# Eight 64 KB weight transfers on two queues in place of one 512 KB transfer ahead of the activations

## The chip, the core and the metric

The kernel runs on one core of a Trainium2 chip. The metric is the device time of one launch in microseconds: 327.43 us, the median of 3 runs (327.39 to 327.58).

## What is computed

There are 128 samples `x[b]` of 128 channels by 1024 time steps, eight weight matrices of 128 by 128, and for each sample an index that chooses one of the eight. Each sample is multiplied by its matrix and added to the product; everything is float32.

```python
# x: (128, 128, 1024); subjects: (128,) of 0..7; weights: (8, 128, 128)
w = weights[subjects]
out = x + jnp.einsum('bct,bcd->bdt', x, w)
```

The input is 67.1 MB of samples and 0.5 MB of weights, the output 67.1 MB.

## The kernel before, in words

The work goes in 64 tiles of `G = 2` samples. A tile lies in one of `SLOTS = 23` slots of the on-chip memory, each 1 MB (`xs`), is multiplied into one of two PSUM buffers (`ps`), and the sum is written over the sample itself, from where it is stored. The order is written out by hand with semaphores, engine by engine:

- **SyncE (SP) issues the loads**, on its own DMA queue (q1 in the profile). Its first transfer is `w_all`, all eight matrices in one (L148): the matrix index becomes the middle dimension on the chip, so that each piece of the transfer is one matrix row, 512 bytes. Then the loop at L149 issues each sample as a transfer of 512 KB (L158, inside the helper `transfer`, whose instruction is at L59). `ROWS = 4` makes each piece read four neighbouring rows, 16 KB. Tiles 0 to 2 are issued at once; from tile 3 (`LEAD = 3`) SP first waits until the tile three before has landed (L155, L156), and from tile 23 until the slot's former tile has been stored (L152, L153). At the end SP waits for the last stores (L222).
- **ScalarE (ACT) issues** the index vector `given` (L127) as its first transfer, and later all stores (L212 to L217), on its own DMA queue (q10). It does nothing else.
- **VectorE (DVE)** fills `zeros` (L129), brings the indices into range (L139 to L143), and for every tile adds product and sample (L210).
- **GpSimd (POOL)** reads the indices, waits once for `w_all` (L186: `s_wall` at 16, since each transfer adds 16 to its semaphore), and copies the chosen matrix of every sample to one of four small buffers (L189). The copy of a tile from the third on waits for the tile's load as well (L193).
- **TensorE (PE)** starts with `IDLE = 3` multiplications of zeros (L132), which are recorded as six. Each sample then is two multiplications of 512 columns (L199). Tile 0 is done as two single samples, so that the first one can begin when sample 0 has landed; it has a semaphore of its own, `s_first`.

The loads, the stores and the index vector all share the core's 16 DMA engines.

Of the kernel before, what the change touches and what calls it, by code (L numbers as in the profile page):

```python
# [36 lines left out]
DMA = 16  # L40
# [7 lines left out]
ROWS = 4  # L48
# [3 lines left out]
def transfer(nc, engine, out, in_):  # L52

    later, nc._always_lower_symbolic_ap = nc._always_lower_symbolic_ap, False
    ins, outs = engine.lower_ap_dma(in_), engine.lower_ap_dma(out)
    nc._always_lower_symbolic_ap = later
    return engine.add_instruction(  # L59
        mybir.InstDMACopy(  # L60
            name=nc.get_next_instruction_name(),
            engine=engine.engine,
            ins=ins,
            outs=outs,
            mode="Copy",
            cce_op=ALU.bypass,
            queue=QUEUES[engine.engine],
        )
    )


@with_exitstack
def kernel(
    ctx: ExitStack,
    tc: tile.TileContext,
    x: bass.AP,
    subjects: bass.AP,
    weights: bass.AP,
    out: bass.AP,
):  # L80
    nc = tc.nc
    B, C, T = x.shape
    S, _, D = weights.shape
    NT = B // G

    def sbuf(name, *shape, dtype=F32):
        return ctx.enter_context(nc.sbuf_tensor(name, list(shape), dtype)).ap()

    given, near, wrap, index = (
        sbuf(name, 1, B, dtype=I32) for name in ("given", "near", "wrap", "index")  # L90
    )
    w_all = sbuf("w_all", C, S, D)
    ws = [sbuf(f"w{i}", C, 1, D) for i in range(W_SLOTS)]
    zeros = sbuf("zeros", C, N)
    xs = [sbuf(f"x{i}", C, G, T) for i in range(SLOTS)]
    ps = [
        ctx.enter_context(nc.psum_tensor(f"ps{i}", [D, G, T], F32)).ap() for i in range(P_SLOTS)
    ]

    s_given = tc.alloc_semaphore("s_given")  # L100
    s_wall = tc.alloc_semaphore("s_wall")
    s_index = tc.alloc_semaphore("s_index")
    s_zeros = tc.alloc_semaphore("s_zeros")
    s_copied = tc.alloc_semaphore("s_copied")
    s_product = tc.alloc_semaphore("s_product")
    s_added = tc.alloc_semaphore("s_added")
    s_slot = [tc.alloc_semaphore(f"s_slot{i}") for i in range(SLOTS)]


    s_first = tc.alloc_semaphore("s_first")  # L110

    def loaded(i):

        k, turn = i % SLOTS, i // SLOTS
        if i == 0:
            return [(s_first, DMA), (s_slot[0], DMA)]
        return [(s_slot[k], TURN * turn + DMA * G - (TURN - 2 * DMA if k == 0 else 0))]

    def stored(i):

        if i == 0:
            return [(s_first, 2 * DMA), (s_slot[0], 2 * DMA)]
        return [(s, count + DMA) for s, count in loaded(i)]

    with tc.tile_critical():  # L125

        nc.scalar.dma_start(given, subjects.rearrange("(o b) -> o b", o=1)).then_inc(s_given, DMA)  # L127

        nc.vector.memset(zeros, 0.0).then_inc(s_zeros, 1)  # L129
        nc.tensor.wait_ge(s_zeros, 1)  # L130
        for _ in range(IDLE):
            nc.tensor.matmul(  # L132
                ps[P_SLOTS - 1][:, G - 1, :N], zeros[:, :D], zeros, start=True, stop=True
            )

        nc.vector.wait_ge(s_given, DMA)
        nc.vector.tensor_scalar(near, given, -S, S - 1, ALU.max, ALU.min).then_inc(s_index, 1)  # L139
        nc.vector.wait_ge(s_index, 1)  # L140
        nc.vector.tensor_scalar(wrap, near, 0, S, ALU.is_lt, ALU.mult).then_inc(s_index, 1)  # L141
        nc.vector.wait_ge(s_index, 2)
        nc.vector.tensor_tensor(index, near, wrap, ALU.add).then_inc(s_index, 1)  # L143
        nc.gpsimd.wait_ge(s_index, 3)

        nc.sync.dma_start(w_all, weights.rearrange("s c d -> c s d")).then_inc(s_wall, DMA)  # L148
        for i in range(NT):  # L149
            k = i % SLOTS  # L150
            if i >= SLOTS:
                for s, count in stored(i - SLOTS):  # L152
                    nc.sync.wait_ge(s, count)  # L153
            elif i >= LEAD:
                for s, count in loaded(i - LEAD):  # L155
                    nc.sync.wait_ge(s, count)  # L156
            for g in range(G):
                transfer(  # L158
                    nc,
                    nc.sync,  # L160
                    xs[k][:, g, :],
                    x[i * G + g].rearrange("(a r) t -> a (r t)", r=ROWS),
                ).then_inc(s_first if i + g == 0 else s_slot[k], DMA)


        units = [(0, g, g + 1) for g in range(G)] + [(i, 0, G) for i in range(1, NT)]
        for u, (i, g0, g1) in enumerate(units):
            k = i % SLOTS
            p = ps[i % P_SLOTS]

            if i < P_SLOTS:
                nc.tensor.wait_ge(*loaded(i)[g0])
            for g in range(g0, g1):
                b = i * G + g
                if b % R == 0:
                    _, subject = nc.values_load_multi_w_load_instructions(  # L178
                        index[0:1, b : b + R],
                        engines=[mybir.EngineType.Pool],  # L180
                        min_val=0,
                        max_val=S - 1,
                        skip_runtime_bounds_check_because="the index is clamped on the chip above",
                    )
                if b == 0:
                    nc.gpsimd.wait_ge(s_wall, DMA)  # L186
                if i >= P_SLOTS and g == g0:
                    nc.gpsimd.wait_ge(s_added, u - P_SLOTS + 1)
                copy = nc.gpsimd.tensor_copy(  # L189
                    ws[b % W_SLOTS], w_all[:, bass.ds(subject[b % R], 1), :]  # L190
                )
                if i >= P_SLOTS and g == g0:
                    copy.wait_op(*loaded(i)[0], "sem-ge")  # L193
            copy.then_inc(s_copied, 1)

            nc.tensor.wait_ge(s_copied, u + 1)
            for g in range(g0, g1):
                for t in range(0, T, N):
                    mm = nc.tensor.matmul(  # L199
                        p[:, g, t : t + N],  # L200
                        ws[(i * G + g) % W_SLOTS][:, 0, :],
                        xs[k][:, g, t : t + N],
                        start=True,
                        stop=True,
                    )
            mm.then_inc(s_product, 1)

            mine = xs[k][:, g0:g1, :]
            nc.vector.wait_ge(s_product, u + 1)
            nc.vector.tensor_tensor(mine, p[:, g0:g1, :], mine, ALU.add).then_inc(s_added, 1)  # L210
            nc.scalar.wait_ge(s_added, u + 1)
            transfer(  # L212
                nc,
                nc.scalar,
                out[i * G + g0 : i * G + g1].rearrange("g d t -> d g t"),
                mine.rearrange("d (o g) t -> d o (g t)", o=1),
            ).then_inc(s_first if u == 0 else s_slot[k], DMA)  # L217


        for i in range(NT - SLOTS, NT):  # L220
            for s, count in stored(i):
                nc.sync.wait_ge(s, count)  # L222
# [27 lines left out]
```

## Time and profile before

| | before |
|---|---|
| median of the runs | 327.43 us (327.39 to 327.58) |
| the profiled execution: own time, span from first to last instruction | 327.13 us, 325.4 us |
| PE, DVE, POOL busy | 240.0, 148.0, 34.3 us |
| DMA | 134.85 MB, mean 414 GB/s |
| `w_all`: issue, time to issue, from issue to landing | at 0.97 us, 0.44 us, 4.3 us |
| first four samples: issue starts | 1.46, 2.08, 2.71, 3.35 us |
| median packet on a DMA engine: 512 bytes, 4 KB, 8 KB, 16 KB | 27, 159, 311, 616 ns |

The first rows are the page's and the times'. The issue starts come from the timeline, the packet rows from the trace's record of every DMA packet: a packet is one contiguous piece of a transfer, and it belongs to one of the 16 engines. The profile was taken on one execution, whose own time lies 0.3 us under the median; 1.7 us of it lie outside its span.

### The profile page before, as it was taken

To read this page: it belongs to the slowest core of one execution; us is meant where nothing else is said; L and a number is where in the kernel's file an instruction comes from. 1 tells how busy PE (TensorE), PEld (TensorE's weight loads), DVE (VectorE), ACT (ScalarE), POOL (GpSimd) and SP (SyncE) were. 2 spreads that over 40 slices of the span, in tenths; PEclk is the share of its full clock that TensorE was granted. 3 is DMA by queue.
4 is the path that set the end of the run, shared out by engine and by line. 5 is a ranking of instruction groups with operands and counts; after the bars stand their busy time and mean duration, and the time that the engine had idled before them with its cause. 6 is when DMAs were issued, how large, how long until landed. Compare 5 with 4: busy or idle time off the path is not lost.

```text
span 325.4 us, 1637 instructions
## 1 busy us (share of the span) xinstructions
PE 240.0 (74%) x518; PEld 94.3 (29%) x518; DVE 148.0 (45%) x69; POOL 34.3 (11%) x132
## 2 busy tenths in 40 slices
PE   7999978989999989889889889887866867000000
PEld 3344323333333333333333333332322322000000
DVE  1466654555555555555555555555254453100000
POOL 1011111111111111111111111111011010000000
PEclk9999999999999999999999999999999999655555
DMA  7999999999999999999999999999999999999994
GB/s 258 401 426 431 419 428 418 421 425 425 427 427 423 421 430 422 426 425 423 426 421 423 422 431 419 429 420 431 421 430 427 418 424 426 425 429 423 428 425 203
DMA packets 16554, 134.85 MB, mean 414 GB/s; under 512 B 3105, under 2 KB 4130, under 8 KB 4386
## 3 DMA queue, kind: packets, MB, share of 16 engines
q1 hardware_dynamic: 7184, 67.64, 49.7%
q10 hardware_dynamic: 9362, 67.11, 49.2%
q8 instruction: 4, 0.07, 0.1%
q14 instruction: 4, 0.03, 0.0%
HBM read 67.63 MB, written 67.11 MB: 414 GB/s over the span
## 4 chain that ended last, share of the span: by engine, by line
PE 39%; DVE 21%; issue 17%; POOL 4%; DMA 2%; POOLq 1%; SPq 1%
PE ps L199 39%; DVE x L210 21%; POOL w L189 4%; DMA x<-in_x_dram 2%; POOLq L189 1%; SPq L59 1%; POOLq L178 0%; SPq L148 0%; SPq L246 0%; SPq L125 0%
## 5 line engine op out<-in xcount | busy, mean ns | idle before, releaser
L199 PE MATMUL ps<-x,w 128*128 128x512 f32 x512 | 235.2, 604 | 34.1 <-POOL w L189 33.2
L210 DVE TENSOR_TENSOR x<-ps,x 128x2048 f32<-128x2048 f32 (+1 forms) x65 | 146.8, 2259 | 128.2 <-PE ps L199 128.2
L199 PEld LDWEIGHTS ps<-x,w 128*128 128x128 f32 x512 | 92.5, 189 | 176.8 <-issue 91.8
L189 POOL COPY w<-w_all 128x128 f32 x128 | 34.1, 296 | 237.4 <-DMA x<-in_x_dram 220.6
L132 PE MATMUL ps<-zeros 128*128 128x512 f32 x6 | 4.7, 956 | 1.7 <-DVE zeros L129 1.7
L132 PEld LDWEIGHTS ps<-zeros 128*128 128x128 f32 x6 | 1.9, 329 | 3.7 <-issue 2.1
L129 DVE MEMSET zeros<- 128x512 f32 x1 | 0.5, 485 | 1.1 <-SPq L125 1.1
L139 DVE TENSOR_SCALAR near<-given 1x128 int32<-1x128 int32 x1 | 0.2, 215 | 0.6 <-DMA given<-in_itok_B_dram 0.6
L143 DVE CUSTOM_DVE_ANT_0 index<-near,wrap 1x256 uint16<-1x256 uint16 x1 | 0.3, 281 | 0.0
L141 DVE TENSOR_SCALAR wrap<-near 1x128 int32<-1x128 int32 x1 | 0.2, 216 | 0.0
L237 POOL MEMSET const-float32-0.0<- 128x1 f32 x1 | 0.1, 99 | 0.2 <-issue 0.2
L237 POOL MEMSET const-bfloat16-1.0<- 128x1 bf16 x1 | 0.1, 102 | 0.0
L237 POOL MEMSET const-uint8-127<- 128x1 uint8 x1 | 0.1, 102 | 0.0
L237 POOL MEMSET const-float32-1.0<- 128x1 f32 x1 | 0.1, 99 | 0.0
## 6 DMA issues: line engine op xcount, KB each, us to landing
x<-in_x_dram SPq DMA_DIRECT2D x128, 512.0 KB, 11.8
out_dram<-x ACTq DMA_DIRECT2D x63, 1024.0 KB, 41.6
out_dram<-x ACTq DMA_DIRECT2D x2, 512.0 KB, 11.3
w_all<-in_L_cond_weights_dram SPq DMA_DIRECT2D x1, 512.0 KB, 4.3
given<-in_itok_B_dram ACTq DMA_DIRECT2D x1, 0.5 KB
```

The lines of the kernel that those rows point to most:

```text
L59: return engine.add_instruction(mybir.InstDMACopy(name=nc.get_next_instruction_name(), engine=engine.engine, ins=ins, outs=outs, mode="Cop ...
L129: nc.vector.memset(zeros, 0.0).then_inc(s_zeros, 1)
L132: nc.tensor.matmul(ps[P_SLOTS - 1][:, G - 1, :N], zeros[:, :D], zeros, start=True, stop=True)
L139: nc.vector.tensor_scalar(near, given, -S, S - 1, ALU.max, ALU.min).then_inc(s_index, 1)
L141: nc.vector.tensor_scalar(wrap, near, 0, S, ALU.is_lt, ALU.mult).then_inc(s_index, 1)
L143: nc.vector.tensor_tensor(index, near, wrap, ALU.add).then_inc(s_index, 1)
L189: copy = nc.gpsimd.tensor_copy(ws[b % W_SLOTS], w_all[:, bass.ds(subject[b % R], 1), :])
L199: mm = nc.tensor.matmul(p[:, g, t : t + N], ws[(i * G + g) % W_SLOTS][:, 0, :], xs[k][:, g, t : t + N], start=True, stop=True,)
L210: nc.vector.tensor_tensor(mine, p[:, g0:g1, :], mine, ALU.add).then_inc(s_added, 1)
L237: nc = _bacc.Bacc("TRN2", target_bir_lowering=False, num_devices=1)
```

## The change

The one transfer of `w_all` on SP's queue (L148) goes. A helper `load_matrix` moves one matrix, with pieces of four rows (2 KB) on the side that is read. Matrices 4 to 7 are issued by ACT, directly after the index vector. Matrices 0 to 3 are issued by SP, between sample 0 and sample 1, so that sample 0 is now SP's first transfer. All eight count on `s_wall`, and POOL's wait before its first copy asks for all of them.

```diff
+    def load_matrix(engine, m):
+        transfer(
+            nc,
+            engine,
+            w_all[:, m, :],
+            weights[m].rearrange("(a r) d -> a (r d)", r=ROWS),
+        ).then_inc(s_wall, DMA)
+
     with tc.tile_critical():
 
         nc.scalar.dma_start(given, subjects.rearrange("(o b) -> o b", o=1)).then_inc(s_given, DMA)
+        for m in range(S // 2, S):
+            load_matrix(nc.scalar, m)
...
-        nc.sync.dma_start(w_all, weights.rearrange("s c d -> c s d")).then_inc(s_wall, DMA)
         for i in range(NT):
...
                 ).then_inc(s_first if i + g == 0 else s_slot[k], DMA)
+                if i + g == 0:
+                    for m in range(S // 2):
+                        load_matrix(nc.sync, m)
...
-                    nc.gpsimd.wait_ge(s_wall, DMA)
+                    nc.gpsimd.wait_ge(s_wall, DMA * S)
```

## The prediction

> **What bounds the kernel now.** I read the page's slices first, then its DMA queues, then the DMA share in short stretches at both ends, then the waits.
>
> ```profile
> DMA  7999999999999999999999999999999999999994
> GB/s 258 401 426 431 419 428 418 421 425 425 427 427 423 421 430 422 426 425 423 426 421 423 422 431 419 429 420 431 421 430 427 418 424 426 425 429 423 428 425 203
> ...
> q1 hardware_dynamic: 7184, 67.64, 49.7%
> q10 hardware_dynamic: 9362, 67.11, 49.2%
> ```
>
> The 16 DMA engines are full from the second slice to the last. Loads (q1) and stores (q10) together take 98.9% of 16 engines' time: 0.989 x 325.4 = 321.8 us of 325.4. Only 3.6 us per engine are left. The page's chain of waits names PE (39%) and DVE (21%), but PE has 240.0 us of work and DVE 148.0; the chain crosses them because each tile must pass them, while tiles come as fast as the DMA brings them. So I count everything in DMA time. Where are the 3.6 us?
>
> ```profile
> 1.50:2.00 0.50, 0.33 (x1) 0.33 (x2) 0.12 (x1) 0.00 (x0) 1.00 0.00 1
> 2.00:2.50 0.50, 0.50 (x1) 0.18 (x1) 0.28 (x2) 0.00 (x0) 1.00 0.53 139
> 2.50:3.00 0.50, 0.50 (x2) 0.31 (x1) 0.43 (x2) 0.00 (x0) 1.00 0.38 81
> 3.00:3.50 0.50, 0.50 (x1) 0.03 (x1) 0.00 (x0) 0.00 (x0) 1.00 0.91 266
> 3.50:4.00 0.50, 0.50 (x2) 0.34 (x1) 0.00 (x0) 0.00 (x0) 1.00 1.14 350
> ...
> 6.00:300.00 294.00, 235.64 (x513) 92.45 (x512) 146.84 (x65) 33.56 (x126) 0.96 1.01 424
> 300.00:320.00 20.00, 0.00 (x0) 0.00 (x0) 0.00 (x0) 0.00 (x0) 0.50 1.01 426
> 320.00:323.00 3.00, 0.00 (x0) 0.00 (x0) 0.00 (x0) 0.00 (x0) 0.50 0.37 156
> ```
>
> The last two columns are DMA share and GB/s. Nothing moves before 2 us (the first load packet starts at 2.07). From 2.0 to 3.0, while `w_all` starts, the engines are about half idle; from 3.5 on they are full until 320. The last stretch shows engines finishing unevenly: by the increments of the last store's semaphore they end between 320.6 and 323.8 us, mean 321.7, and the second latest is 322.7. One straggling engine sets the end.
>
> So a change in the first microseconds is worth what it moves the start of continuous DMA work, engine by engine, and above all on the engines that end late.
>
> **What the Trainium skill says.** "DMA: Bandwidth & Descriptors", section "Issuing engines are not separate DMA queues": transfers issued by sync and by scalar run on the same 16 engines; a second issuer only saves issue time. The trace agrees: the two queues' shares add to 98.9% and never beyond. The same page, "Specifications", has 512 bytes as the smallest transfer at line rate. The trace disagrees: a 512-byte packet takes 27 ns (19 GB/s on one engine) where an 8 KB packet takes 311 ns (26.3 GB/s). "Perfetto Trace Analysis", section "DMA Instruction — HWDGE (DVE, Sync)": a descriptor generator shared by the issuing sequencers is locked for exclusive use, and the recorded issue time contains the wait for the lock. The trace shows no such price so far: an SP issue takes 0.47 us after a wait and about 0.60 back to back, both with an ACT issue running beside it (at 143.5 and 144.0 us the first is 0.473) and without.
>
> **The change part by part.** For the start I use the packet records. In the kernel before, averaged over engines, `w_all` is through at 4.35 us and sample 0 at 5.67; at that moment sample 1 begins. After, the same 1 MB has to be through before sample 1 begins, in another order. So the gain is 5.67 minus the time at which sample 1's packets start.
>
> *Removed:* `w_all`, 1024 packets of 512 bytes, 64 per engine: 64 x 27 ns = 1.73 us per engine, plus about 0.5 us of idle time in its first microsecond, together the 2.28 us from 2.07 to 4.35.
>
> *Added, packets:* 8 matrices x 32 pieces of 2 KB = 256 packets, 16 per engine. No 2 KB packet is in this trace. The line through 512 bytes (27 ns) and 4 KB (159 ns) is 8 ns + 0.037 ns per byte, so 84 ns each, 1.34 us per engine. From above: on the chip side each piece is still four rows of 512 bytes; if those count, 4 x 27 = 108 ns and 1.73 us, no saving. Samples speak for the first: their 16 KB pieces are four chip rows of 4 KB, and take 616 ns, not 4 x 159 = 636. I take 1.34. From below, at the 26.6 GB/s of a 16 KB packet, 77 ns, 1.23 us. Seven more semaphore increments per engine at 9 ns are 0.06 us.
>
> *Added, issues.* Each small transfer still has to be issued. On ACT the four follow `given` (0.92 to 1.45 us); ACT's first store comes at 10.25, so these four lie beside nothing that waits: cost nothing. Without that cover (8.8 us) they would delay the first store. On SP the four lie between sample 0 and sample 1, and behind them are queued all other loads. The issue of a sample costs 0.60 + 0.04 us back to back, `w_all` cost 0.44 + 0.05. A matrix through the same helper should lie between: 0.49 to 0.64; I take 0.60. SP then: sample 0 at 0.97 for 0.47 + 0.04, matrices from 1.48, sample 1 at 1.48 + 4 x 0.60 = 3.88 us (before: 2.08).
>
> *When sample 1 flows.* `w_all` took 2.07 - 0.97 = 1.10 us from issue to first packet. So sample 1 starts at 3.88 + 1.10 = 4.98 us. Are the engines free by then? They have 2.07 + sample 0 at 2 x 0.611 + matrices 1.34 + 0.07 for increments = 4.70 us. If up to 0.5 us of starting idle time stays, 5.2. The matrices arrive at both queues every 0.6 us, each pair worth 0.34 us of engine time, so the later ones leave the engines partly idle, which hides the 2 KB price. The idle time that `w_all` had is in part replaced by idle time for want of issues.
>
> *Sum:* 5.67 - 4.98 = 0.69 us of DMA time earlier. Range of this step: SP at 0.49 per matrix gives 3.44 + 1.10 = 4.54, so the engines' 4.70 decides and the gain is 0.97; SP at 0.64 and idle time 0.2 us longer gives 0.35.
>
> *What follows it.* SP issues the next samples every 0.64 us for 1.24 us of engine work each, so DMA stays full; the wait for tile 0 ahead of tile 3 (SP waited there until 8.4 us) moves with the data. POOL's wait now ends with matrix 3: issue 3.28 + 1.10 + 0.17, plus 0.43 from packet to visible increment (as `w_all`: 4.35 to 4.79 on average) = about 5.0 against 5.29 before. PE is occupied by the multiplications of zeros until 6.42 anyway. Earlier stores take DMA time from loads, but the sum of bytes is unchanged.
>
> *Against the metric.* The profiled execution is 327.13 us, so 326.4 by this sum; taken off the median 327.43 it is 326.7. I forecast **326.7 us**, just beyond the 0.2% (0.65 us) that I count as what a measurement of this kernel can tell from no change.
>
> **Rivals.**
>
> *The straggler gains too.* By the records, four engines had one 16 KB packet of about 1.35 to 1.55 us instead of 0.61 between 4.5 and 7 us, and end sample 0 as late as 6.43 against the mean of 5.67. If engines wait idle for sample 1, this lag is wiped out, and the engine that ends last may start up to 0.75 us better than the mean. That is 326.7 - 0.6 = 326.1. Against it: such long packets may come back with the next samples.
>
> *It does nothing.* The first packet of sample 1 comes later than 1.10 us after its issue, because a transfer behind others in the generator is not like the first one, or sample 0 meets the slow start that `w_all` met. With 0.5 us of this: 327.2. For it: the engines already lagged behind issue at the start. Against it: the idle gap ahead of sample 1 can absorb a slow sample 0.
>
> *Slower: the two issuers share one generator.* If SP's and ACT's issues exclude each other during these nine, SP advances once per two issues of 0.47, every 0.94 us: sample 1 at 0.97 + 5 x 0.94 = 5.67, flowing at 6.77, which is 1.10 us later than before: 328.5. It decides from 0.72 us per issue (0.97 + 5 x 0.72 + 1.10 = 5.67). For it: the skill's lock, and long runs of issues on both sides at once with empty rings do not occur before. Against it: the overlapping pairs cited above, and `given` beside `w_all` at 0.92 us, at 0.53 and 0.44.
>
> **How the numbers follow.** The forecast has 0.56, of it 0.34 beyond 0.2% faster and 0.22 inside; the straggler 0.20, faster; nothing 0.12, same; slower 0.12. So faster 0.54, same 0.34, slower 0.12. The range goes from the straggler's case with a tenth to spare, 326.0, over the "nothing" case with a bit of noise, 327.6, and leaves out the slower case and the best end.
>
> **What would show it.** Right: sample 1 issued near 3.9 us and flowing near 5.0; ACT's four done by 3.9; a weight packet near 84 ns; the DMA share at 1 from about 5 us; the end earlier by what the start gained. Wrong: SP issues of 0.8 us or more in the first 5 us; the last engine ending at 323.8 although the mean is earlier; or a DMA share under 1 somewhere after 6 us.

## The result and the profile after

| | before | after |
|---|---|---|
| median | 327.43 us (326.88 to 327.58, 6 runs) | 328.90 us (328.68 to 329.06, 6 runs) |
| profiled execution: own time, span | 327.13, 325.4 us | 328.95, 327.2 us |
| increments of the last store: mean, latest engine | 321.68, 323.83 us | 323.07, 325.64 us |

The ratio is 1.0047, with a 95% interval of 1.0034 to 1.0060: the change costs 1.5 us where 0.7 us of gain was forecast, and lies 1.3 us beyond the upper end of the range.

The page of the changed kernel, its slices and its two DMA queues:

```profile
DMA  6999999999999999999999999999999999999994
GB/s 216 377 420 435 419 420 427 424 422 427 425 425 425 421 425 429 423 427 425 424 426 419 429 421 429 422 425 425 427 425 432 424 422 422 426 427 427 425 427 182
...
q1 hardware_dynamic: 6336, 67.38, 49.5%
q10 hardware_dynamic: 9554, 67.38, 49.2%
```

From the third slice on the slices differ by no more than 10 GB/s, up or down, until the last one. The first two slices moved 216 and 377 GB/s instead of 258 and 401: over 8.2 us each that is 0.54 MB less, and at the later 425 GB/s this takes 1.3 us to make up. Nearly the whole difference arises in the first 16 us.

The timeline of SP's queue in the changed kernel (start, length, what was issued, how often):

```profile
0.97 0.55 SPq L60 DMA_DIRECT2D x<-in_x_dram  x1
1.57 2.68 SPq L60 DMA_DIRECT2D w_all<-in_L_cond_weights_dram  x4
4.29 1.24 SPq L60 DMA_DIRECT2D x<-in_x_dram  x2
```

Sample 1 was issued at 4.29 us (3.88 was expected). The DMA share and GB/s (last two columns) of the changed kernel in the first microseconds:

```profile
3.00:3.50 0.50, 0.50 (x1) 0.02 (x1) 0.00 (x0) 0.00 (x0) 1.00 1.33 492
3.50:4.00 0.50, 0.50 (x2) 0.33 (x1) 0.00 (x0) 0.00 (x0) 1.00 0.29 98
4.00:4.50 0.50, 0.50 (x2) 0.10 (x1) 0.00 (x0) 0.00 (x0) 1.00 0.92 266
4.50:5.00 0.50, 0.50 (x2) 0.23 (x1) 0.00 (x0) 0.00 (x0) 1.00 0.93 324
5.00:5.50 0.50, 0.50 (x2) 0.25 (x1) 0.00 (x0) 0.00 (x0) 1.00 0.75 238
5.50:6.00 0.50, 0.50 (x1) 0.08 (x1) 0.00 (x0) 0.00 (x0) 1.00 1.50 463
6.00:7.00 1.00, 0.97 (x2) 0.00 (x0) 0.00 (x0) 0.00 (x0) 1.00 0.89 270
7.00:8.00 1.00, 0.00 (x0) 0.00 (x0) 0.00 (x0) 0.00 (x0) 1.00 0.85 264
8.00:10.00 2.00, 1.09 (x3) 0.65 (x4) 0.00 (x0) 1.00 (x4) 1.00 1.07 303
```

A packet counts here in the stretch in which it begins, so single half microseconds swing between 0.29 and 1.50. Two things are to be seen. At 5.0 to 5.5 us the share is 0.75: the engines run dry before sample 1 comes (spread over the time that they took, the packets fill 0.76 of this half microsecond and 0.65 of the next). From 6 to 10 us the share is near 1 again, but only 264 to 303 GB/s move. The share counts the time that packets took, so a packet that waits counts as busy. The kernel before moved 360 to 418 GB/s in these microseconds:

```profile
6.00:8.00 2.00, 1.45 (x4) 0.56 (x4) 0.00 (x0) 0.46 (x2) 1.00 0.88 360
8.00:10.00 2.00, 2.00 (x6) 0.88 (x5) 1.01 (x1) 0.00 (x0) 1.00 0.99 410
10.00:12.00 2.00, 1.71 (x5) 0.56 (x4) 1.44 (x2) 0.00 (x0) 1.00 1.06 418
```

And the end, where the kernel before had a share of 0.37 between 320 and 323 us:

```profile
300.00:320.00 20.00, 0.00 (x0) 0.00 (x0) 0.00 (x0) 0.00 (x0) 0.50 1.01 426
320.00:323.00 3.00, 0.00 (x0) 0.00 (x0) 0.00 (x0) 0.00 (x0) 0.50 0.79 330
323.00:325.40 2.40, 0.00 (x0) 0.00 (x0) 0.00 (x0) 0.00 (x0) 0.50 0.08 34
```

The rate before it is the same 426 GB/s; the work of the start is only done later.

The packet records say what fills that time: 16 KB packets of 0.9 to 2.2 us instead of 0.616. I use three sums per engine. **Idle** is the 12 us from 2 to 14 us less the mean time in which packets were on the engines. **Excess** is the time of all packets that began by 14 us beyond 9, 27, 84, 159, 311 or 616 ns by their size. **Lag** is the data moved by 16 or 40 us that is missing against the kernel before, divided by 425 GB/s; data that an experiment adds is not counted as moved.

| | idle | excess | 16 KB packets over 0.9 us | lag at 16, at 40 us |
|---|---|---|---|---|
| before | 0.58 us | 0.76 us | 9 | 0, 0 |
| after | 0.92 us | 1.96 us | 35 | 1.20, 1.34 us |

Idle is 0.34 us worse and excess 1.20 us; the cheaper weight packets give back some 0.3. That leaves 1.2 of the 1.39 us by which the mean of the last increments moved. The lag, counted without any price per packet, says the same. The latest engine moved by 1.81.

### The profile page after: what moved, and what is told of

Its sections match the earlier page's. It is cut to its first block, busy times and chain, and to the rows that moved or that the text cites. A ratio compares the mean times of both kernels' runs of the same rounds, so it can differ in the third digit from the quotient of the medians.

```text
span 327.2 us, 1644 instructions
## 1 busy us (share of the span) xinstructions
PE 241.3 (74%) x518; PEld 95.1 (29%) x518; DVE 148.0 (45%) x69; POOL 34.0 (10%) x132
## 4 chain that ended last, share of the span: by engine, by line
PE 42%; DVE 19%; issue 17%; POOL 4%; DMA 1%; POOLq 1%; SPq 1%
PE ps L212 42%; DVE x L223 19%; POOL w L202 4%; DMA w_all<-in_L_cond_weights_dram 1%; POOLq L202 1%; SPq L60 1%; POOLq L191 0%; SPq L259 0%; SPq L134 0%
```

## The experiments

The theories: **A**, sample 1 is issued late and the engines run dry; **B**, sample transfers that begin, or begin again, on all engines at once get long packets, and the 512-byte pieces in front of them kept the kernel before free of these; **G**, every further transfer in the start costs long packets; others stand with their runs. All 18 runs in one table; ratios are to the kernel before on the same chip. Idle, excess and lag come from one profiled execution each, which need not be a typical one: that of e1 took 327.65 us, the least of its 19 runs, that of h5 327.10, that of f3 330.23.

| run | median us | ratio (95%) | idle | excess | lag at 16, at 40 us |
|---|---|---|---|---|---|
| e1_x1_ahead | 328.41 | 1.0036 (1.0027 to 1.0045) | 0.82 | 1.56 | 0.67, 0.90 |
| e2_all_act | 328.66 | 1.0043 (1.0028 to 1.0058) | 0.72 | 1.51 | 0.57, 1.21 |
| e3_one_behind | 328.01 | 1.0021 (1.0014 to 1.0027) | 0.25 | 1.26 | 0.20, 0.22 |
| e4_one_act | 327.37 | 1.0000 (0.9992 to 1.0008) | 0.29 | 0.69 | -0.36, -0.05 |
| f1_rows1 | 328.68 | 1.0039 (1.0025 to 1.0054) | 0.68 | 1.34 | 0.59, 0.94 |
| f2_other_rows | 328.72 | 1.0045 (1.0031 to 1.0059) | 1.05 | 1.23 | 0.63, 1.18 |
| f3_change_rows1 | 329.14 | 1.0046 (1.0032 to 1.0060) | 0.82 | 2.00 | 1.58, 1.59 |
| f4_split_in_front | 329.75 | 1.0063 (1.0045 to 1.0082) | 1.63 | 1.86 | 2.09, 2.29 |
| g1_tiny_act | 327.80 | 1.0014 (1.0007 to 1.0020) | 0.20 | 1.08 | 0.18, 0.30 |
| g2_tiny_sp | 329.05 | 1.0054 (1.0037 to 1.0070) | 0.81 | 1.78 | 1.41, 1.40 |
| g3_one_late | 330.30 | 1.0088 (1.0071 to 1.0105) | 0.70 | 1.40 | 0.25, 1.61 |
| g4_eight_late | 329.49 | 1.0068 (1.0051 to 1.0085) | 0.62 | 1.22 | 0.00, 1.42 |
| h1_apart | 329.12 | 1.0049 (1.0034 to 1.0064) | 1.14 | 1.23 | 1.35, 1.85 |
| h2_gap | 329.66 | 1.0065 (1.0050 to 1.0081) | 1.53 | 1.81 | 2.15, 2.16 |
| h4_change_512 | 328.70 | 1.0039 (1.0024 to 1.0054) | 0.93 | 1.46 | 1.08, 1.33 |
| h5_halves | 327.78 | 1.0013 (1.0004 to 1.0022) | 0.47 | 0.97 | 0.06, 0.17 |
| k1_lead2 | 330.08 | 1.0097 (1.0074 to 1.0120) | 1.64 | 2.33 | 2.44, 2.75 |
| k2_gap_small | 330.05 | 1.0095 (1.0076 to 1.0113) | 1.81 | 0.43 | 2.61, 2.73 |

### Parts of the change undone

**e1_x1_ahead**, from the changed kernel:

```diff
-                if i + g == 0:
+                if i == 0 and g == 1:
                     for m in range(S // 2):
                         load_matrix(nc.sync, m)
```

> The changed kernel, with SP's four matrices behind sample 1 instead of in front of it. Theory A (late issue: sample 1 waits behind four issues and the DMA engines run dry): sample 1 is issued near 1.6 us, the engines go from sample 0 to sample 1 without a gap, and some 0.5 us of the 1.5 come back: about 328.3; all of it would be 327.4. Theory B (lockstep: engines that start sample transfers all at the same moment get long 16 KB packets): the engines still leave sample 0 together, the long packets between 6 and 11 us stay: 328.3 or more, with at least 1 us per engine of excess over 0.616 us per packet in the first 14 us. Theory C (it is the 2 KB pieces or the eight semaphore rounds themselves): no gain, 328.9.

Measured: 328.41. Sample 1 was issued at 1.56 us and began near 3.9 us, before sample 0 had ended; 29 long packets stayed. But the four issues now stand ahead of sample 2, as SP's queue shows:

```profile
2.18 2.72 SPq L60 DMA_DIRECT2D w_all<-in_L_cond_weights_dram  x4
4.94 4.18 SPq L60 DMA_DIRECT2D x<-in_x_dram  x6
```

So the late issue was moved on by one sample and not taken away, and idle time fell from 0.92 us to no less than 0.82. The two ratios, 1.0036 and 1.0047, lie 0.4 us apart, and their intervals overlap. How much the late sample 1 costs is not settled by this run.

**e2_all_act**, from the changed kernel: `for m in range(S)` on ACT, and SP's three lines are out.

> The changed kernel with all eight matrices issued by ACT, none by SP. Theory A: SP's loads are issued without a gap, DMA is full from 2.3 us on and only the matrices are slow to be issued (until 6.6 us): the start is better than in the kernel before, 326.6 to 327.0. Theory B: long packets stay, since nothing but small packets at wide spacing mixes the engines: 327.6 to 328.3. Theory C: 328.9.

Measured: 328.66, slower than B's range. With SP's queue free of weights no sample is issued late, and the loss is still 1.4 us. Theory A alone falls, though only half of the loss belongs to the start: the lag is 0.57 us at 16 us and 1.21 at 40. The second half is taken up under e4. The stretches of e2:

```profile
4.00:6.00 2.00, 2.00 (x4) 0.58 (x2) 0.00 (x0) 0.00 (x0) 1.00 1.23 367
6.00:8.00 2.00, 0.33 (x1) 0.00 (x0) 0.00 (x0) 0.00 (x0) 1.00 0.72 266
8.00:10.00 2.00, 0.00 (x0) 0.00 (x0) 0.00 (x0) 0.00 (x0) 0.69 1.06 422
```

The same dip to 266 GB/s, now between 6 and 8 us, and with PE, DVE and POOL doing next to nothing, so the compute engines' work is not needed for it.

**e3_one_behind**, from the kernel before: the line of `w_all` (L148) moved behind sample 0.

```diff
-        nc.sync.dma_start(w_all, ...).then_inc(s_wall, DMA)
...
+                if i + g == 0:
+                    nc.sync.dma_start(w_all, ...).then_inc(s_wall, DMA)
```

> The kernel before with its one transfer of 512-byte pieces put behind sample 0 on SP's queue: the order of the change without its splitting. Theory A: one issue of 0.45 us stands ahead of sample 1, no gap: within 0.3 us of 327.4. Theory B: 64 small packets per engine come behind sample 0 and unlock the engines as in the kernel before: also 327.4; if the order itself locks them, 328.3 or more. Theory C: 327.4.

Measured: 328.01. The order alone costs 0.7 us although idle time fell to 0.25: nine packets of sample 0 took 0.97 to 1.18 us, and nine of sample 1, near 5.5 us, 1.05 to 1.73 us. Both theories had expected this one too low.

**e4_one_act**, from the kernel before: the same line issued by `nc.scalar`, behind the index vector.

> The kernel before with its one transfer of 512-byte pieces issued by ACT, behind the index vector; SP begins with sample 0. Theory A: no gap, both queues have work from 2.3 us on: 326.6 to 327.0, the best of the four. Theory B: the two queues' packets mix and unlock the engines: the same 326.6 to 327.0; if not, 328. Theory C: 327.0.

Measured: 327.37, ratio 1.0000. Here the weights' small pieces came from the other queue between samples 0 and 1, and the excess is about the kernel before's. The idle time it saved (0.29 us) did not show in the end: at 16 us the kernel was 0.36 us ahead, at 40 us no longer. Its first weight copy on POOL began at 11.08 us, and its first store was issued at 16.56 us instead of 10.25. This seems to cost time. From 16 to 34 us the kernel before, e4 and g4 (whose first store was issued at 35.07 us) moved:

```profile
16.00:34.00 18.00, 18.00 (x43) 7.96 (x42) 12.29 (x6) 2.67 (x10) 1.00 1.01 425
16.00:34.00 18.00, 18.00 (x43) 7.89 (x42) 10.92 (x6) 2.67 (x10) 1.00 1.00 416
16.00:34.00 18.00, 3.81 (x5) 1.70 (x6) 0.18 (x1) 1.00 (x4) 0.51 1.00 394
```

At the same share of 1, g4's loads without stores beside them went at 394 GB/s, with 16 KB packets of 0.66 us on average instead of 0.616; why is open. In these kernels, the later the first store, the more was lost between 16 and 40 us: 0.1 us in the changed kernel (12.83 us), 0.3 in e4, 0.6 in e2 (23.65 us), 1.4 in g4. So a late start of compute seems to cost something here through late stores; no run changes the stores alone.

**f4_split_in_front**, from the changed kernel: SP's four matrices in front of sample 0.

> The splitting alone: eight transfers with 2 KB pieces, four on each queue, but SP's four in front of sample 0, where the one transfer stood. The engines have only 0.17 us of work per issue of 0.64 us, and sample 0 is issued at 3.5 us and flows at 4.8 instead of 4.35: 0.5 us late by that alone. Theory B: few and widely spaced small packets leave the engines in step, so long packets come as in the changed kernel: 328.7 or more. If the place behind sample 0 is what does it (theory E): 327.9.

Measured: 329.75. The place behind sample 0 is not what does it, so theory E falls. The splitting alone, in the old place, is the worst of all placements in the start: 1.63 us idle, because 64 KB per issue do not feed the engines, and then a common start of the samples near 5.06 us with 1.86 us of excess.

**h4_change_512**, from the changed kernel: `weights[m]` in place of `weights[m].rearrange("(a r) d -> a (r d)", r=ROWS)`.

> The changed kernel with every matrix in pieces of one row, 512 bytes, as in the kernel before; order, queues and the eight transfers stay. If the 2 KB pieces themselves save what the packets' prices say (1.73 against 1.34 us per engine): it makes no difference to the end, since the engines run dry at that time; 328.9, or 0.2 us less dry time. Theory B: 64 small packets per engine, but sample 1 still restarts all engines together: 328.7 to 329.2.

Measured: 328.70, 0.2 us under the changed kernel with overlapping intervals. The 2 KB pieces are neither the gain nor the loss.

### What the long packets depend on

**f1_rows1**, from e2, and **f3_change_rows1**, the same line in the changed kernel:

```diff
-                    x[i * G + g].rearrange("(a r) t -> a (r t)", r=ROWS),
+                    x[i * G + g].rearrange("(a r) t -> a (r t)", r=1 if i < LEAD else ROWS),
```

> The kernel of e2 (all matrices on ACT, 328.66 us), with the first six samples read in pieces of one row, 4 KB, instead of four rows. Theory B1 (lockstep with 16 KB pieces[...]): [...]the samples follow each other at 1.3 us from the start: 327.2 or less. Theory B2 (lockstep at the memory that is read): also changes, direction open. Theory D (the first 3 MB are slow whatever their shape, a cold start): the samples still take 1.8 us each, 328.7.

> The changed kernel (328.90 us) with the first six samples in pieces of one row, 4 KB. Theory B1: the excess of the long packets (1.1 us per engine more than in the kernel before) goes, the late sample 1 (0.45 us) stays: 327.7 to 327.9. Theory D: 328.9.

Measured: 328.68 and 329.14, with excesses of 1.34 and 2.00. Quarter-size packets become long just the same (4 KB packets of 0.55 to 1.5 us that began between 4.2 and 5.8 us in f1). B1 falls: the size of the samples' pieces is not it. Theory D, that the first 3 MB are slow whatever their shape, meets both numbers. Against it stand e4, which loads the same first samples with an excess of 0.69, and below k2 and k1.

**f2_other_rows**, from e2: the first six samples are read with `s=ROWS + 1` and `[:, :ROWS, :]` over the flattened rows, so a row is skipped after every four.

> The kernel of e2, with the first six samples read from other addresses: after every four rows one row is skipped, so that an engine's pieces lie 20 KB apart and not 16 KB; sizes, engines and places on the chip stay, and these six samples hold other data. Theory B2 (conflict at the memory that is read, from the equal power-of-two distances): the long packets mostly go, 327.4 or less. Theory B1 (conflict at the on-chip side) and theory D (cold start): nothing changes, 328.7.

Measured: 328.72, excess 1.23 against e2's 1.51. Other distances do not take the long packets away, so B2 in this form falls; D's number is met again.

**g1_tiny_act** and **g2_tiny_sp**, from the kernel before:

```diff
+        for m in range(S):
+            transfer(nc, nc.scalar, pad[:, m, :], weights[m][:16, :]).then_inc(s_pad, DMA)
```

for g1 behind the index vector; for g2 `range(S // 2)` and `nc.sync`, behind sample 0.

> The kernel before, with eight added transfers of 8 KB each (16 rows of 512 bytes, one row per engine, into memory that nobody reads) issued by ACT behind the index vector. They move 0.01 us of data per engine each, so this counts transfers without bytes. Theory B (engines in step are slow; the one transfer of 512-byte pieces in front keeps them apart): nothing changes, within 0.3 us of 327.3. Theory G (every further transfer that is issued while the queues start up costs long packets of other transfers): about what lies between one and eight weight transfers on ACT, 1.3 us: 328.0 to 328.6.

> The kernel before, with four such transfers of 8 KB issued by SP behind sample 0. Sample 1 is then issued at 4.6 us and can flow at 5.7, when the engines are just through with sample 0 (5.67). Theory B and the late issue alone: 327.3 to 327.6. Theory G: half of what eight cost, 327.8 to 328.2.

Measured: g1 327.80, +0.4 us for eight transfers; g2 329.05, +1.7 us for four. The number is not what counts, and G falls as the main cause. But B had expected no more than 327.6 for both, so it missed too: in g2 it had reckoned with engines that are only just through with sample 0. That a dry spell and a second start of the samples count as well was added to B after this run. In g2 sample 1 was issued at 4.61 us, as in the changed kernel, the engines ran dry, and the same dip followed. The stretches of g2 around the dip:

```profile
6.00:8.00 2.00, 2.00 (x6) 0.77 (x4) 0.00 (x0) 0.13 (x1) 1.00 1.10 385
8.00:10.00 2.00, 2.00 (x6) 0.76 (x4) 1.23 (x1) 0.00 (x0) 1.00 1.01 270
10.00:12.00 2.00, 0.58 (x2) 0.30 (x2) 1.23 (x1) 0.00 (x0) 1.00 0.99 385
```

**g3_one_late** from e4 and **g4_eight_late** from e2: ACT waits for `loaded(LEAD - 1)` before the weights.

> The kernel of e4 (one transfer of all matrices, on ACT; 327.37), which ACT now issues only when tile 2 has landed, near 9 us: the first six samples run alone, with nothing that keeps the engines apart. Multiplications begin later; nothing that sets the end depends on that. Theory B: long packets for several microseconds, 328.3 or more. Theory G: the fewest transfers in the start, 327.0 to 327.4.

> The kernel of e2 (eight matrices on ACT; 328.66), which ACT now issues only when tile 2 has landed. Theory G, if the cost belongs to the first microseconds: 327.3 or less; if it belongs to the transfers whenever they come: 328.5. Theory B: 328.3 or more, from the six samples that run alone.

Measured: 330.30 and 329.49. With nothing but samples in the first 9 us the excess is 1.40 and 1.22, where G wanted the best start of all. But the lag at 16 us is only 0.25 and 0.00 us, as no weights took time. It comes to 1.61 and 1.42 by 40 us, from the second loss shown under e4: the first copy on POOL began at 46.3 us in g3, where the weights landed 34 us after their issue (see below), and at 29.8 in g4, and no store could go before. So these two medians meet B's number for another reason and do not speak for it; the excess does. G wins nothing by that: its numbers, 327.4 and 327.3 or 328.5, are missed.

**h2_gap**, from the kernel before, behind sample 0:

```diff
+                if i + g == 0:
+                    nc.sync.wait_ge(s_wall, DMA)
```

> The kernel before, in which SP waits, behind sample 0, until the weights have landed (5.3 us), before it issues sample 1. No transfer is added and none is moved; the engines run dry after sample 0 (5.67 on average) and start again together with sample 1, issued at 5.3 and flowing at 6.5 to 6.9: 0.9 to 1.2 us of dry time. If dry time is all: 328.3 to 328.6. Theory B: the common restart brings long packets 2 to 3 us later, another 0.6 to 1.1 us: 329.0 to 329.6, with an excess of 1.5 us or more.

Measured: 329.66. This adds and moves no transfer; it only makes the engines dry once. They began again together at 6.66 us, 1.0 us after the kernel before had begun sample 1, and the excess rose to 1.81. Dry time and excess, 1.0 + 1.05, account for 2.05 of the 2.27 us, and the lag of 2.15 us at 16 us says the same. The stretches of h2:

```profile
6.00:8.00 2.00, 2.00 (x4) 0.81 (x3) 0.00 (x0) 0.55 (x3) 1.00 0.86 262
8.00:10.00 2.00, 2.00 (x5) 0.68 (x4) 0.82 (x1) 0.00 (x0) 1.00 1.25 361
10.00:12.00 2.00, 1.08 (x3) 0.19 (x1) 1.29 (x2) 0.00 (x0) 1.00 0.67 254
```

It shows the dip of the changed kernel without any part of the change.

**k2_gap_small**, from h2: behind the wait, the weights once more, in 512-byte pieces into memory that nobody reads.

```diff
+                    nc.sync.dma_start(pad, weights.rearrange("s c d -> c s d")).then_inc(s_pad, DMA)
```

> The kernel h2 with the dry spell (329.66; 1.8 us of excess per engine in the first 14 us), in which SP, before sample 1, issues the whole weight transfer of 512-byte pieces once more, into memory that nobody reads. That adds 1.73 us of work per engine and 0.5 us of issue. Theory B: small pieces at the restart set the engines apart, as they do at the start of the kernel before; the excess falls to 1.2 us or less, and the time rises by 0.7 to 1.3 us instead of 1.7 to 2.2: 330.3 to 331.0. If small pieces in front do not help (another reason for the good start of the kernel before): excess 1.7 us or more, 331.3 to 331.9.

Measured: 330.05; the ratio rose by 0.003, 1.0 us, for 1.73 us of added work. The excess is 0.43, with one 16 KB packet over 0.9 us (34 in h2). The stretches of k2, to be held against those of h2:

```profile
6.00:8.00 2.00, 2.00 (x4) 0.81 (x3) 0.00 (x0) 0.41 (x2) 1.00 0.47 140
8.00:10.00 2.00, 1.18 (x3) 0.19 (x1) 0.78 (x1) 0.00 (x0) 1.00 1.22 441
10.00:12.00 2.00, 1.20 (x3) 0.68 (x4) 0.45 (x1) 0.00 (x0) 1.00 0.97 393
```

The dry time and the restart with small pieces take the first stretch; after that the samples run at full rate at once. By the lag, 1.73 us of added work cost 0.46 us (2.61 against 2.15). That is B's second half: with small pieces at the restart the long packets stayed away. It rests on one trace, and no run put the same bytes there in large pieces; in h2, where the first 512 KB of the restart were a sample's 16 KB pieces, long packets came at once (6.66 us) and again in sample 3 (9.5 us).

**h1_apart**, from e2: in front of sample 0, 256 KB on eight engines only.

```diff
+        transfer(
+            nc,
+            nc.sync,
+            xs[SLOTS - 1][:32, :, :].rearrange("c g t -> c (g t)"),
+            x[:2].rearrange("b (a r) t -> (b a) (r t)", r=32)[:, : 4 * G * T],
+        ).then_inc(s_pad, DMA)
```

> The kernel of e2 (long packets cost it 1.6 us per engine in the first 14 us beyond what 27, 84, 159 and 616 ns would give), with one added transfer in front of sample 0 that is spread over eight of the 16 engines only, 32 KB on each: those eight begin sample 0 up to 1 us after the others. It adds 1.2 us of work to eight engines, so the time alone says little; the excess does. Theory B (engines in step): the excess falls to 1.0 us or less, and the time stays within 0.8 us of e2's 328.66 though work was added. Theory S (what counts is that samples come first and nothing else, or the number of transfers): the excess stays at 1.6, the time rises to 329.3 or more.

Measured: 329.12, 0.46 us over e2, and excess 1.23 (a 32 KB packet counted at 1.22 us) against 1.51. The time is on B's side, the excess is not, and the lag at 16 us is 1.35 against 0.57, a difference of 0.78 us for 0.62 us of added work. So "in step" in the sense of two halves a fixed time apart is not shown to be the reason.

**k1_lead2**, from the changed kernel: `LEAD = 2`.

> The changed kernel with LEAD = 2: samples 4 and 5 are issued only when tile 0 has landed (near 9 us), so that fewer transfers are queued in the start; later it also holds back loads by one tile. Theory B (the common restart with sample 1 makes the long packets): those between 7 and 11 us stay, excess 1.7 us or more in the first 14 us, 328.9 or some more for dry time behind sample 3. Theory I (long packets come when descriptors of further transfers arrive, about 1.1 us after each issue): the packets of 1.1 to 2.2 us that begin near 8.8 us, after the issue of sample 5 at 6.85, go; excess 1.4 us or less, 328.5 or less.

Measured: 330.08. The issues of samples 4 and 5 were gone from the start, and the long packets were not: sixteen of over 1 us began between 5.7 and 8.4 us, and after the next dry spell many more came, until 17 us. Theory I falls, and what B says holds a second time in one run: dry again (a share of 0.65 from 12 to 14 us), long packets again. That is late for a cold start (D).

**h5_halves**, from the kernel before: half of the matrices on each queue, in front of all else.

> A version that might beat both: the kernel before with its weight transfer in two halves of four matrices, 512-byte pieces, one half on each queue, in front of all else. The engines were half idle in the first microsecond of the weights; two queues may fill them: 0.2 to 0.4 us, 327.0 to 327.2. Theory B says the engines stay apart as in the kernel before, so no long packets come in: not over 327.5.

Measured: 327.78, slightly slower than the kernel before and above B's bound of 327.5: with 512-byte pieces in front of all else, 17 long packets came all the same, most of them near 5.3 to 6.3 us (excess 0.97). The profiled execution, at 327.10, does not show the loss of the median. No version in this study beats the kernel before.

## Why the prediction was wrong

**The bound was right.** All time was DMA time, and the end moved with the start: the mean last increment by 1.39 us for 1.2 us of worse start. What had fallen behind in the first 16 us (1.20 us) was not made up later.

**The prices were right as medians, not as sums.** The median 2 KB packet took 84 ns, as forecast, and ACT's four issues were done at 3.98 us and delayed nothing. But sample 0's packets took 0.79 us on average, not the 0.611 of the sum, and the sixteen 2 KB packets of an engine together 0.37 us more than 16 x 84 ns, which is about what they were to save (1.73 - 1.34 = 0.39 us).

**The late sample 1 was mis-sized.** SP's matrices took 0.58, 0.77, 0.60 and 0.60 us, and sample 0 0.55 instead of 0.47: issue at 4.29 instead of 3.88. From issue to the first packet it took 1.46 us (5.75 - 4.29), not the 1.10 of the very first transfer. The forecast 4.98 became 5.75 at the earliest engine, against 5.67 on average before, so the 0.69 us of gain turned into none. These two terms make the rival "it does nothing", which had named the longer way from issue to packet.

**The step that failed** is "so DMA stays full", to which the sum gave no price. After sample 1 the share was indeed near 1, but the packets were long. I took a busy engine for one that moves bytes at 26.6 GB/s. The 1.20 us of excess is the larger part of the loss, and no term of the sum and no rival had it as a cost; the straggler's rival only remarked that long packets "may come back with the next samples". The trace of before held a hint that I turned the wrong way round: four packets of 1.35 to 1.55 us near 5 us. I put them down as a lag that a common restart would wipe out. h2 shows that a common restart made more of them: 34 instead of 9.

**The slower rival** had the right sign by the wrong mechanism: with both queues issuing at once one SP issue took 0.77 us and the others 0.58 to 0.60, far from the 0.94 that sharing a generator in turns would give. Its evidence was read too kindly, though: right after the cited issue of 0.473 us comes one of 0.83 (144.0 us), and from 90 to 140 us SP's issues beside ACT's took 1.0 to 4.1 us. No run here says why.

**POOL's wait** ended at 8.47 us, not near 5.0: one 2 KB packet of the weights began at 6.34 us and took 1.51 us, and the last increment came at 8.30. The prediction held this wait to be without effect. It made the first store 2.6 us later, and the lag grew by 0.14 us between 16 and 40 us; that the late stores are the reason is argued from e4, e2 and g4.

**What stays open.** Shown is: a dry spell followed by sample transfers on idle engines gives stretches of 250 to 300 GB/s in the 5 us that follow (h2, g2, k1), a start with a sample in front does so too (e2, g3), and with 512-byte pieces at the restart the stretches were absent (k2, one trace). In the changed kernel both are at work, the sample in front and the restart with sample 1; how the 1.20 us divide between them is not measured apart. Piece size (f1, f3), the distances at which the pieces are read (f2), the number of transfers (g1) and later issues (k1) are not the reason. Why small pieces help is not settled: that they set the engines apart is argued only, h1 speaks for little of it, and in e3, with small pieces directly in front of sample 1, and in h5, with small pieces in front of everything, long packets came nevertheless. What inside the transfer engines or the memory makes a packet wait was not seen.

## What to carry to other kernels

Where DMA bounds a kernel, read GB/s beside the DMA share: a share of 1 with two thirds of the usual rate is a loss that no sum of packet prices contains. Watch when the first store goes out: here loads without stores moved 394 GB/s at a share of 1, where loads and stores together moved 425. Do not let the queues of loads run dry in the start for the sake of a shorter first transfer: count the issues that stand between two large transfers, at the 0.6 us and 1.1 to 1.5 us that this trace shows for an issue and for its way to the engines. A small transfer in front of everything may do work that its own price does not tell, so try its removal alone before removing it with other things.

## What the hardware did that I had not expected

- After a common restart, 16 KB packets took up to 2.2 us instead of 0.616, for about 5 us (changed kernel, 6 to 11 us), and 4 KB packets took up to 1.5 us in f1.
- A transfer of many small pieces on one queue starves beside 16 KB packets on the other. The lines for the weights in the lists of DMA issues, first of g3, then of e2 (issuer, count, KB each, median us to landing):

```profile
w_all<-in_L_cond_weights_dram ACTq DMA_DIRECT2D x1, 512.0 KB, 33.9
```

```profile
w_all<-in_L_cond_weights_dram ACTq DMA_DIRECT2D x8, 64.0 KB, 7.6
```

  The same 512 KB that landed in 4.3 us at the start took 33.9 us between loads. The Trainium skill, "DMA: Bandwidth & Descriptors", section "Queues, rings and completion order", says that an engine changes between queues packet by packet. What the page calls a packet is a group, of typically 9 to 17 descriptors; the trace records single pieces. From the first small piece of g3 at 15.9 us to the last at 45.5, 699 pieces of 16 KB began beside the 1024 small ones, about two for three. At 0.645 and 0.029 us each, their means in this stretch, that is 30 us of work per engine: the two queues took turns, as the page says, and by the number of pieces rather than by bytes.
- The way from issue to first packet was 1.10 us for the first transfer of the kernel before, 1.33 us for sample 0 in the changed kernel (2.30 - 0.97), and 1.46 us for its sample 1, with the engines waiting.
